# Mask constants copied by DVE and POOL instead of ACT, with a new order of issue, in a sliding-window transformer block

## The chip, the cores and the metric

The kernel runs on one core of one Trainium2 chip. The time is device microseconds of one execution. Before the change it is 662.07 us, the median of 3 runs (661.29 to 662.28).

The engines have short names here: PE is TensorE (matmuls; PEld is its weight load), DVE is VectorE, ACT is ScalarE, POOL is GpSimd, and SP is SyncE, which issues the transfers. "Lnnn" is a line of the kernel before.

## What is computed

The input is 4 sequences of 2,048 rows with 256 features. One block of a transformer is applied: layer normalisation, attention over a sliding window, residual; layer normalisation, a feed-forward net whose weights are rounded to -1, 0 and 1, residual.

```python
def attn(x, Wq, Wk, Wv, Wo):             # 16 heads of 16
    q, k, v = proj(x, Wq), proj(x, Wk), proj(x, Wv)
    allowed = (j <= i) & (j > i - 64)    # 64 keys back
    bias = where(allowed, 0, -inf)
    attn = softmax(q @ k.T * 0.25 + bias)
    return (attn @ v) @ Wo.T

def ffn(x, W1, b1, W2, b2):
    q = lambda W: clip(round(W / (mean(abs(W)) + 1e-5)), -1, 1)
    return relu(x @ q(W1).T + b1) @ q(W2).T + b2

x = hidden
x = x + attn(layernorm(x), Wq, Wk, Wv, Wo)
x = x + ffn(layernorm(x), W1, b1, W2, b2)
```

## The kernel before

**Tiling.** The rows are cut into 32 chunks of 256 (`C`), 8 to a sequence. Each chunk goes through the same stages: load, normalise (`norm_in`), projections to q, k and v (`project`), a stacked operand (`stack`), row maxima (`maxima`), attention weights (`weights`), values (`values`), output projection (`wo_out`), and the two layers of the feed-forward net (`ffn1`, `ffn2`). Precision is kept by splitting a float32 number into a high and a low float16 half: ACT writes the high half, and DVE or POOL subtracts to give the low one.

**The stacks and the mask.** The mask is folded into the matmul of the scores. There are three buffers `st`, used in turn by the chunks (chunk 0, 3, 6 and so on use the first). Each has three planes of 16 heads x 256: plane 0 for the queries, planes 1 and 2 for the keys, at two offsets of the window. Partitions 64 to 111 get the q and k halves of the chunk by transfers (L703). The other partitions hold constants: `qcon` in plane 0 and `kcon` in planes 1 and 2, which make scores outside the window very negative. These constants are written once for each buffer, in `stacks`: 12 copies of 128 x 1024 each (4 for each plane), 36 in all. Before the change ACT makes the copies of plane 1 (L334, 12 in all) and DVE those of planes 0 and 2 (L337, 24 in all). A chunk's transfers into its buffer come after the copies. When they have landed, DVE moves the keys of plane 1 into plane 2 (L714, L716, L719). Then PE computes scores for the maxima (L749), DVE reduces them (L757, twice a chunk), the maxima go through a transpose (L771) and a transfer (L777) into the last row of plane 0, and PE computes the scores again for the exponentials (L792).

**The low half of the weights.** `weights` has two forms. In one, ACT writes the exponentials into a buffer `r` (L802), casts the high half (L805), and POOL subtracts (L807). In the other ACT works in the bank of PSUM (L811, L813) and DVE subtracts (L815). The method `pick` chooses by how loaded the engines are so far.

**The start.** Weights are loaded and prepared while the first chunks are normalised and projected. The feed-forward weights need the mean of their absolute values: four sums on ACT (L460), a matmul (L466), a threshold on DVE (L469 to L472), the rounding on DVE (L482, L484), for the first weight a subtract on POOL (L489) and bias columns copied by POOL (L496), and transposes on PE (L499, L510). Thirty filler tasks of four small matmuls each (L424) keep PE busy when it has nothing else.

**What sets the order.** Nothing is left to a scheduler on the chip. `Lanes` runs the whole program once in a model at build time: each task is a generator which says which engine it needs and for how long (`yield "A", 0.9` is ACT for 0.9 us), which buffer it takes, and what it waits for. Among the tasks that could start, the planner takes the one that starts first (within `TOL`), and among those the one of lowest priority number. That number is made from `PRIO`, `SLOPE` (times the chunk), and `EARLY` for the first three chunks. The order in which the planner picks tasks is the order of the instructions on each engine and in SP's queue, fixed by explicit dependencies. An engine never takes a later instruction first. So a constant of the planner can move any instruction of the kernel; the durations in `yield` are only the planner's assumptions.

Of the kernel before, what the change touches and what calls it, by code (L numbers as in the profile page):

```python
# [19 lines left out]
D = 256  # L20
# [16 lines left out]
PARTS = slice(64, 112)  # L37
R = 113
BIGH = 60000.0
PRIO = {'norm': 23.33, 'proj': 25.05, 'max': 13.47, 'att': 27.65, 'val': -28.15, 'wo': 28.21, 'ffn': -22.66, 'ffn2': 41.64, 'mask': 31.19, 'prep': 14.07}  # L40
SLOPE = {'norm': 0.0, 'proj': 0.024, 'max': 0.0, 'att': 0.045, 'val': -0.116, 'wo': 0.043, 'ffn': 0.052, 'ffn2': -0.228, 'mask': -0.25, 'prep': 0.0}
BUFS = {'xt': 11, 'ln': 2, 'xT': 3, 'zT': 4, 'qk': 2, 'pp': 6, 'op': 2, 'o': 2, 'h': 7, 'r': 5, 'bank': 5, 'lin': 5, 'sp': 1, 'tp': 3, 'pv': 4}
BANKS = ("lin", "tp", "pv")
EARLY = {'norm': (0.0, 0.0, 1.08), 'proj': (0.0, 0.0, 0.0), 'max': (10.44, 0.0, 0.0), 'att': (0.0, 0.0, 0.0), 'val': (0.0, 15.88, 0.0), 'wo': (-6.94, 0.0, 0.0), 'ffn': (10.96, 3.26, -1.28), 'ffn2': (0.0, 2.05, -3.47), 'mask': (0.72, 0.0, 0.0), 'prep': (0.0, 0.0, -1.0)}
TOL = 0.0
FIRST = 0.0
BOOST = 3.34
CHAIN = ('PE', 'DVE', 'Activation', 'Pool', 'SP')
LAT = {"P": 0.2, "A": 0.17, "D": 0.15, "G": 0.13, "S": 0.97}
TAU = 35.06  # L50
DMAF, DLAT = 1.15, 0.83
WINDOW = 3.4133
WT = {'P': 0.93, 'A': 1.17, 'D': 1.05, 'G': 1.07, 'S': 0.0}


class Lanes:
# [21 lines left out]
    def put(self, pool):  # L78
        self.slots[pool].append(self.cur[0])
        self.wake(("get", pool))  # L80
        if pool == "sp":
            self.cur[1] += BOOST
        if pool in BANKS:
            self.cur[1] += BOOST
            self.slots["bank"].append(self.cur[0])
# [11 lines left out]
    def pick(self, options):  # L97

        top = max(self.load[e] * WT[e] for e in "PADG")
        cost = [sum(t * math.exp((self.load[e] * WT[e] - top) / TAU) for e, t in o) for o in options]  # L100
        return cost.index(min(cost))
# [47 lines left out]
    def run(self):  # L149
        while self.ready:  # L150
# [21 lines left out]
            if not could:  # L172
                break
            first = min(x[0] for x in could) + TOL
            start, _, task = min((x for x in could if x[0] <= first), key=lambda x: (x[1], x[0]))
# [4 lines left out]
            if what == "get":  # L180
# [3 lines left out]
                if arg in BANKS or arg == "sp":  # L184
                    task[1] -= BOOST
            elif what == "S":
# [17 lines left out]
def kernel(ctx: ExitStack, tc: tile.TileContext, x, Wq, Wk, Wv, Wo, W1, b1, W2, b2, out):  # L204
    nc = tc.nc
    B, S, _ = x.shape
# [33 lines left out]
    def wait(*key):  # L240
        return ("wait", key)

    def signal(*key):
        lanes.signal(key)
# [3 lines left out]
    def start(kind, c, gen, k=0):  # L248
        early = EARLY[kind][int(c)] if c < 3 else 0.0
        lanes.add(c * (1 + SLOPE[kind]) + PRIO[kind] + early + 0.001 * k, gen)  # L250

# [8 lines left out]
    st = [const.tile([128, 3, H, C], HP, name=f"st{i}") for i in range(NQ)]  # L260
# [66 lines left out]
    def stacks(i):  # L327
        yield wait("masks")
        for k in range(3):
            for h in range(0, H, 4):  # L330
                src = (qcon if k == 0 else kcon[:, k - 1]).unsqueeze(1).to_broadcast([128, 4, C])
                if k == 1:
                    yield "A", 0.9
                    nc.scalar.copy(st[i][:, k, h:h + 4], src)  # L334
                else:
                    yield "D", 0.35
                    nc.vector.tensor_copy(st[i][:, k, h:h + 4], src)  # L337
        signal("used", i - NQ)

# [642 lines left out]
    for i in range(NQ):  # L982
        start("mask", i, stacks(i))
# [28 lines left out]
```

## Time and profile before

| what | value |
|---|---|
| median of 3 runs | 662.07 us (661.29 to 662.28) |
| the profiled execution | 662.08 us |
| its span | 660.3 us |
| mean granted PE clock | 0.987 |
| L334, ACT copies of the mask, 12 | 12.6 us, 1066 ns each, from 15.8 to 37.6 us |
| L337, DVE copies of `kcon`, 12 | 6.6 us, 566 ns each (411 to 1377) |
| L337, DVE copies of `qcon`, 12 | 5.1 us, 472 ns each |
| L757, first reduce of maxima | starts at 43.0 us, the second at 46.7 us |
| first L792, scores for the exponentials | 53.2 us |
| L807, low halves of the weights on POOL, 242 | 283.4 us, 1193 ns each |
| L815, the same on DVE, 14 | 9.3 us, 685 ns each |
| L703, q and k into a stack, 192 transfers | 3.9 us from issue to landing (median) |

The span is the time from the first to the last instruction in the profiled execution; a run's time is 1.8 us longer. The page gives the span in 40 slices of 16.5 us. PE's row shows when the kernel is filled:

```profile
PE   8777789999999999999999999999999999999997
PEclk9978889999999999999999999999999999999999
```

Each digit is the busy share of a slice in tenths, or the granted clock in tenths of full speed. From the seventh slice on (99 us) PE is over 90% busy until the last. Before that it is not, and its clock is granted in part only. In the groups of instructions "<-" stands between what is written and what is read, and the last columns tell the idle time of that engine just before the instructions, with what ended it.

### The profile page before, as it was taken

What the parts mean: (1) busy time and instruction counts of PE and PEld (TensorE: products, weight loads), DVE (VectorE), ACT (ScalarE), POOL (GpSimd) and SP (SyncE); (2) the same over time, 40 slices, a digit from 0 to 9 for tenths busy, and PEclk for the clock granted to TensorE, in tenths of its full rate; (3) what the DMA queues carried; (4) which work ended last, traced back from release to release, by engine and by line L of the source; (5) the groups of instructions that cost most, each with busy time, mean ns of one, the idle gap of its engine ahead of it and who ended that gap; (6) DMA issues with size and microseconds to landing.
All of it is one profiled execution on the core that took longest, in us unless ns stands there. A gap on an engine that the chain in (4) does not pass through costs nothing.

```text
span 660.3 us, 31728 instructions
## 1 busy us (share of the span) xinstructions
PE 626.4 (95%) x13524; PEld 556.2 (84%) x13524; DVE 546.1 (83%) x1145; ACT 534.0 (81%) x1083; POOL 531.5 (80%) x626
## 2 busy tenths in 40 slices
PE   8777789999999999999999999999999999999997
PEld 6656668888899998889988888998898888889986
DVE  7797879987888998888888888889788887878753
ACT  7967788898879886887888789879787978998731
POOL 5355899998979998994998989798969887998630
PEclk9978889999999999999999999999999999999999
DMA  6866478667575878766774755864848776272231
GB/s 184 182 130 135 68 135 150 119 111 142 120 146 110 157 132 123 140 103 141 138 128 97 141 128 113 167 138 99 140 117 148 140 124 142 58 125 65 60 88 49
DMA packets 165037, 81.42 MB, mean 123 GB/s; under 512 B 110880, under 2 KB 162848, under 8 KB 164896
## 3 DMA queue, kind: packets, MB, share of 16 engines
q1 hardware_dynamic: 164896, 79.39, 62.0%
q8 instruction: 106, 1.74, 1.2%
q14 instruction: 35, 0.29, 0.2%
HBM read 11.67 MB, written 8.39 MB: 30 GB/s over the span
## 4 chain that ended last, share of the span: by engine, by line
PE 63%; POOL 12%; DVE 9%; ACT 7%; issue 4%; DMA 3%; SPq 1%; POOLq 0%; ACTq 0%; DVEq 0%
PE bank L917 14%; PE bank L646 8%; PE bank L957 7%; PE bank L958 7%; PE bank L792 6%; POOL pl L807 6%; PE sp L749 5%; PE bank L638 5%; PE bank L882 4%; PE bank L835 3%; PE bank L833 3%; PE bank L834 2%; DVE mx L757 2%; DMA st<-hl 2%; DVE o L851 1%
## 5 line engine op out<-in xcount | busy, mean ns | idle before, releaser
L807 POOL TENSOR_TENSOR pl<-r,ph 128x512 f16<-128x512 f32 x242 | 283.4, 1193 | 23.0 <-ACT ph L805 17.8
L802 ACT ACTIVATE r<-bank 128x512 f32<-128x512 f32 x242 | 137.6, 600 | 23.7 <-PE bank L792 16.0
L805 ACT CAST ph<-r 128x512 f16<-128x512 f32 x242 | 143.7, 629 | 0.8
L917 PE MATMUL bank<-zT,wq 128*128 128x256 f16 x1024 | 125.5, 272 | 0.7 <-DVE o L851 0.7
L957 PE MATMUL bank<-wq,hh 128*128 128x256 f16 x512 | 120.1, 273 | 0.2 <-DVE hl L938 0.2
L757 DVE TENSOR_REDUCE mx<-sp 128x16 f32<-128x1536 f32 x64 | 111.9, 1748 | 10.2 <-PE sp L749 9.9
L958 PE MATMUL bank<-wq,hl 128*128 128x256 f16 x512 | 119.6, 272 | 0.0
L938 DVE SCALAR_TENSOR_TENSOR hl<-bank,hh 128x512 f16<-128x512 f32 x128 | 86.5, 688 | 36.9 <-ACT hh L936 35.5
L917 PEld LDWEIGHTS <-wq 128*128 128x128 f16 x1024 | 97.1, 98 | 12.7 <-DVE o L851 1.2
L936 ACT ACTIVATE hh<-bank 128x512 f16<-128x512 f32 x128 | 75.9, 601 | 31.5 <-PE bank L917 31.2
L792 PE MATMUL bank<-st 114*128 114x64 f16 x2048 | 87.1, 193 | 4.7 <-ACT r L802 2.5
L792 PEld LDWEIGHTS <-st 114*128 114x128 f16 x2048 | 77.6, 98 | 10.0 <-issue 3.3
L833 PEld LDWEIGHTS <-ph 128*128 128x128 f16 x1024 | 82.1, 96 | 4.1 <-DVE o L851 1.0
L834 PEld LDWEIGHTS <-ph 128*128 128x128 f16 x1024 | 80.3, 96 | 4.8 <-issue 3.3
L835 PEld LDWEIGHTS <-pl 128*128 128x128 f16 x1024 | 79.8, 96 | 3.6 <-POOL pl L807 3.3
L851 DVE TENSOR_TENSOR o<-bank,rec 64x128 f32<-64x128 f32 x256 | 73.9, 289 | 8.4 <-POOL rs L542 0.5
L749 PE MATMUL sp<-st 113*32 113x96 f16 (+2 forms) x4608 | 58.7, 202 | 2.8 <-DVE mx L757 1.4
L749 PEld LDWEIGHTS <-st 113*32 113x32 f16 x4608 | 49.2, 96 | 12.1 <-issue 10.5
L683 DVE TENSOR_TENSOR hl<-bank,hl 128x512 f16<-128x512 f32 x64 | 43.8, 689 | 16.6 <-ACT hl L681 15.7
L958 PEld LDWEIGHTS <-hl 128*128 128x128 f16 x512 | 50.0, 98 | 5.0 <-issue 0.3
L957 PEld LDWEIGHTS <-hh 128*128 128x128 f16 x512 | 49.7, 97 | 5.1 <-issue 0.2
L542 POOL TENSOR_TENSOR rs<-rs,mhalf 128x2 f32<-128x2 f32 x64 | 47.1, 736 | 5.3
(118 smaller groups left out, 1518.4 us busy)
## 6 DMA issues: line engine op xcount, KB each, us to landing
st<-hl SPq DMA_DIRECT2D x192, 128.0 KB, 3.9
xt<-in_dram SPq DMA_DIRECT2D x44, 256.0 KB, 4.4
out_dram<-xt SPq DMA_DIRECT2D x32, 256.0 KB, 3.6
ve<-vo SPq DMA_DIRECT2D x32, 136.0 KB, 3.3
ve<-vo SPq DMA_DIRECT2D x60, 68.0 KB, 3.9
oT<-op SPq DMA_TRANSPOSE x64, 3.0
xT<-ht SPq DMA_TRANSPOSE x32, 3.7
st<-mst SPq DMA_DIRECT2D x32, 8.0 KB, 2.3
```

Of the source, the lines that this page charges most:

```text
L749: nc.tensor.matmul(sp[32 * n:32 * n + 32, at:to], st[c % NQ][0:R, 0, h, b * W + q * 32:b * W + q * 32 + 32], window(c, h, b)[0:R, k0:k0 + ...
L757: nc.vector.tensor_reduce(ps_["mx", c][:, w].rearrange("x u p -> x (u p)"), sp.rearrange("x (m k) -> x m k", k=96), AX.X, ALU.max)
L792: nc.tensor.matmul(tp[:, i], window(c, h, b)[0:R + 1], st[c % NQ][0:R + 1, 0, h, b * W:b * W + W], start=True, stop=True)
L802: nc.scalar.activation(pf, tpf, AF.Exp, scale=0.25 / (SW * SW))
L805: nc.scalar.copy(phf, pf)
L807: nc.gpsimd.tensor_tensor(plf, pf, phf, ALU.subtract)
L833: nc.tensor.matmul(pv[:, p, :], ph[:, i, :], v[:, 0, b // 2, p, :], start=True, stop=False)
L834: nc.tensor.matmul(pv[:, p, 0:32], ph[:, i, :], v[:, 1, b // 2, p, 0:32], start=False, stop=False)
L835: nc.tensor.matmul(pv[:, p, :], pl[:, i, :], v[:, 0, b // 2, p, :], start=False, stop=True)
L917: nc.tensor.matmul(ps[:, u], wq1[:, d + d * i, fs], zT[:, i, d], start=n == 0, stop=n == 3)
L957: nc.tensor.matmul(ps[:, t, :], hh[:, f % 2, ts], wq2[:, f, :], start=f == 0, stop=False)
L958: nc.tensor.matmul(ps[:, t, :], hl[:, f % 2, ts], wq2[:, f, :], start=False, stop=f == NF - 1)
```

## The change

It has two parts. In `stacks`, the 12 copies of plane 1 leave ACT: for buffer 0 DVE makes them (4 copies), for buffers 1 and 2 POOL (8 copies). And the planner's constants have other values, so that its order of issue is another throughout.

```diff
-PRIO = {'norm': 23.33, 'proj': 25.05, 'max': 13.47, 'att': 27.65, 'val': -28.15, 'wo': 28.21, 'ffn': -22.66, 'ffn2': 41.64, 'mask': 31.19, 'prep': 14.07}
-SLOPE = {'norm': 0.0, 'proj': 0.024, 'max': 0.0, 'att': 0.045, 'val': -0.116, 'wo': 0.043, 'ffn': 0.052, 'ffn2': -0.228, 'mask': -0.25, 'prep': 0.0}
+PRIO = {'norm': 22.94, 'proj': 25.05, 'max': 12.36, 'att': 27.73, 'val': -26.14, 'wo': 26.43, 'ffn': -22.84, 'ffn2': 39.62, 'mask': 31.7, 'prep': 14.07}
+SLOPE = {'norm': 0.0, 'proj': 0.031, 'max': -0.006, 'att': -0.001, 'val': -0.138, 'wo': 0.105, 'ffn': 0.073, 'ffn2': -0.182, 'mask': -0.25, 'prep': 0.073}
...
-EARLY = {'norm': (0.0, 0.0, 1.08), 'proj': (0.0, 0.0, 0.0), 'max': (10.44, 0.0, 0.0), 'att': (0.0, 0.0, 0.0), 'val': (0.0, 15.88, 0.0), 'wo': (-6.94, 0.0, 0.0), 'ffn': (10.96, 3.26, -1.28), 'ffn2': (0.0, 2.05, -3.47), 'mask': (0.72, 0.0, 0.0), 'prep': (0.0, 0.0, -1.0)}
-TOL = 0.0
+EARLY = {'norm': (1.41, 0.0, 1.08), 'proj': (0.88, 0.27, -1.95), 'max': (10.44, 0.0, 0.0), 'att': (0.0, 0.0, 0.0), 'val': (0.0, 15.66, 0.0), 'wo': (-6.94, 0.0, -5.33), 'ffn': (10.96, 3.26, -1.28), 'ffn2': (0.0, 2.05, -3.47), 'mask': (0.72, 0.0, 0.0), 'prep': (0.0, 0.0, 3.79)}
+TOL = 0.03
 FIRST = 0.0
-BOOST = 3.34
+BOOST = 3.29
...
-TAU = 35.06
-DMAF, DLAT = 1.15, 0.83
+TAU = 34.37
+DMAF, DLAT = 1.14, 0.84
 WINDOW = 3.4133
-WT = {'P': 0.93, 'A': 1.17, 'D': 1.05, 'G': 1.07, 'S': 0.0}
+WT = {'P': 0.95, 'A': 1.19, 'D': 1.05, 'G': 0.96, 'S': 0.0}
...
                 src = (qcon if k == 0 else kcon[:, k - 1]).unsqueeze(1).to_broadcast([128, 4, C])
-                if k == 1:
-                    yield "A", 0.9
-                    nc.scalar.copy(st[i][:, k, h:h + 4], src)
+                if k == 1 and i:
+                    yield "G", 1.3
+                    nc.gpsimd.tensor_copy(st[i][:, k, h:h + 4], src)
                 else:
-                    yield "D", 0.35
+                    yield "D", 0.38 if k == 1 else 0.35
                     nc.vector.tensor_copy(st[i][:, k, h:h + 4], src)
```

`WT` and `TAU` weigh the engines' loads in `pick`: with POOL's weight at 0.96 instead of 1.07, all 256 low halves of the weights go to POOL (L807) and none to DVE (L815). One of 32 second normalisations goes the other way, from POOL and ACT (L580, L581, L584) to DVE (L588). In the number of matmuls nothing changes, and the 120 filler matmuls remain.

## The prediction

> **What bounds the kernel now.** I read the busy shares first, then the same busy times stage by stage, then the chain of waits in order of time.
>
> ```profile
> span 660.3 us, 31728 instructions
> PE 626.4 (95%) x13524; PEld 556.2 (84%) x13524; DVE 546.1 (83%) x1145; ACT 534.0 (81%) x1083; POOL 531.5 (80%) x626
> ```
>
> TensorE (PE) is busy for 95% of the span, so 33.9 us are idle. The stages say where. Columns: stretch, its length, then busy us of PE, PE's weight loads, DVE, ACT, POOL; the granted clock of PE; DMA share; GB/s.
>
> ```profile
> 0.00:16.50 16.50, 13.41 (x96) 9.91 (x96) 13.02 (x45) 12.29 (x35) 8.44 (x26) 1.00 0.64 184
> 16.50:33.00 16.50, 13.19 (x133) 10.87 (x132) 12.93 (x36) 16.50 (x32) 5.61 (x9) 1.00 0.86 182
> 33.00:49.50 16.50, 12.13 (x227) 9.50 (x227) 16.23 (x29) 11.11 (x20) 8.83 (x13) 0.79 0.61 130
> 49.50:66.00 16.50, 13.06 (x311) 10.81 (x315) 11.60 (x21) 12.44 (x27) 9.04 (x10) 0.90 0.63 135
> 66.00:99.00 33.00, 26.04 (x793) 22.77 (x792) 26.41 (x53) 26.54 (x56) 30.20 (x31) 0.90 0.62 102
> 132.00:330.00 198.00, 194.20 (x4337) 175.07 (x4336) 171.84 (x358) 167.56 (x343) 174.75 (x199) 1.00 0.69 130
> 330.00:600.00 270.00, 266.01 (x6151) 238.46 (x6150) 229.01 (x473) 228.06 (x462) 239.36 (x270) 1.00 0.65 124
> ```
>
> From 132 to 600 us PE is idle for 3.80 + 3.99 = 7.8 us of 468: that stretch is bound by PE, and a faster helper gains nothing there. In the first 99 us PE is idle for 21.2 us, and part of its work there is filler (line 424). So a microsecond saved in the head, before PE fills, is a microsecond off the end; the head is where the mask copies lie. There ACT is the full engine from 16.5 to 33 (16.50 of 16.50), and DVE from 33 to 49.5 (16.23 of 16.50). The chain over the first 120 us names the copies; columns are start, length, engine, tile and line:
>
> ```profile
> 15.90 0.93 ACT st L334
> ...
> 27.55 0.63 ACT st L334
> ...
> 28.91 0.93 ACT st L334
> ...
> 30.25 0.93 ACT st L334
> ...
> 36.26 0.93 ACT st L334
> ```
>
> The reader is to see five pieces of line 334 on the chain, 4 x 0.93 + 0.63 = 4.35 us. The other seven copies (of 12) are not on it.
>
> **The change, part by part.**
>
> *Twelve ACT copies go.* Each advances ACT by 0.93 us, so 11.2 us leave ACT, 4.35 us of it from the chain. I don't book 4.35 us, since DVE's order comes next; DVE limits what can be had. DVE works in order. From the threshold step of the first feed-forward weight (line 469, at 17.93 us) to the end of the second maximum of chunk 0 (line 757, ending at 48.43) it takes 30.5 us. In it DVE is idle for 1.09 + 0.41 + 0.51 + 0.16 = 2.2 us, all but 0.16 of it waiting for ACT's line 681. That idle time goes with the copies: -2.2. The step at 17.93 waits for the fourth sum of line 460 on ACT. In the changed order no copy and one weight eviction fewer stand before it (0.93 + 0.27 = 1.2 us). I take half, -0.6, because DVE gets more work before that point (next).
>
> *DVE gets four copies.* They join the chunk-0 stack. A copy takes 0.42 us, and pairs advance by 0.33 (0.75 us for two). In the changed order all eight mask copies of stack 0 are out before the first line 683, while three of the four query copies of stack 2 move behind the threshold. Before the threshold DVE had 0.25 + 0.21 + 1.73 = 2.2 us idle, which covers four more copies (1.3 us) and leaves 0.9; without that cover they cost 1.3. From the threshold to the second maximum I count the instructions in the two issue orders. Line 337 stands 11 times in both, lines 482, 484, 683 and 656 are equal, one batch of statistics (lines 537 and 539, 1.03 us) moves behind, two steps of line 387 (0.4) move ahead, and two of line 567 (0.8) come in: -0.6 us.
>
> *POOL gets eight copies.* The trace has no such copy on POOL. POOL's one-input selects give 0.41 us for 256 elements (line 316) and 0.62 for 512 (line 320), so 0.82 ns an element and 1.04 us for 1,024. The two-input subtract of line 489 takes 1.04 us at least for 512, so 2.1 us is the upper bound. A copy has one input, so I take 1.04: 8.3 us in all (16.7 by the upper bound). POOL idles for 8.45 us before 20.16, then 2.72, 2.59 and some smaller gaps, so its own time is covered for the first four. The last four stand ahead of the third line 489 and of the scaling of chunk 3, and push chunk 3's transposed input about 1 us back, to 40.3 us. Its projection stands behind the first transpose of maxima (line 771), which came at 48.84 us, so this is covered.
>
> What isn't covered is the meeting of POOL and DVE:
>
> ```profile
> 32.03 1.38 DVE L337 COPY st<-kcon 128x1024 f16<-128x1024 f16 x1
> ...
> 34.39 0.41 DVE L337 COPY st<-kcon 128x1024 f16<-128x1024 f16 x1
> ```
> ```profile
> 31.78 1.34 POOL L559 TENSOR_TENSOR ht<-r,ht 128x512 f16<-128x512 f32 x1 [0.64 <-ACT ht L557]
> ```
>
> The first DVE copy ends 0.29 us after the POOL subtract ends at 33.12; the second, with no long POOL work beside it, takes 0.41. It happens again at 38.32 (1.27 us). From 20 to 50 us POOL runs eight long subtracts (four each of lines 489 and 559), and these two meetings cost 0.96 + 0.85 = 1.8 us: 0.23 us a subtract. For the first four POOL copies that is 0.9 us, covered by the 0.9 us left above. For the last four it is +0.9. The bounds are 0 and 4 x 1.04 = 4.2 for each four.
>
> The Trainium skill, "SBUF — State Buffer", "Who interferes with whom", speaks against this part: it says that GpSimd and a VectorE copy in a two-port mode hold one pair of ports in turn, each for its whole instruction, and that the second to come is blocked, not slowed. The rows above agree where the two meet (1.38 and 1.27 us against 0.42). Were each of the eight copies to block DVE for its whole length, the sum would end at about 666 instead of 659.8; the 0.23 us measured per subtract is what decides here.
>
> *The new order of SyncE's queue.* Chunk 1's transpose is no longer second in its pair: its second half (line 564) stands behind all four sums, and the transfer behind the four loads of the second weight (3.24 us) and an input load (0.47). Up to 5 us late; chunk 1's projections follow, with 32 filler matmuls now ahead of them. The cover: chunk 1's stack transfers (line 703) went out at 41.29, 12 us after their data was ready at 29.4, queued behind chunk 3's transpose and a value transfer. Now they stand ahead of both, and chunk 0's six ahead of its value transfer. If the cover failed, the 5 us would come through. I book nothing, since DVE's order (above) sets when the landed stack is used.
>
> *Fourteen subtracts leave DVE.* All 256 low halves of the weights are now made by POOL (line 807), 14 of them formerly by DVE (line 815):
>
> ```profile
> L807 POOL TENSOR_TENSOR pl<-r,ph 128x512 f16<-128x512 f32 x242 | 283.4, 1193 | 23.0 <-ACT ph L805 17.8 <-issue 2.2 <-PE bank L835 1.1
> L815 DVE TENSOR_TENSOR pl<-bank,ph 128x512 f16<-128x512 f32 x14 | 9.3, 685 | 1.0 <-ACT ph L813 0.8
> ```
>
> POOL gains 14 x 1.193 = 16.7 us, DVE loses 9.3, ACT is even within 0.6. From 132 to 600 POOL is busy 414.1 of 468 us (88%); with all 16.7 in it, 92%. PE and its weight loads now wait 2.3 + 3.3 us for line 807, 0.023 us each: 14 more give +0.3. Bounds: 0, and 16.7 if each were on PE's path. One late normalisation moves from POOL and ACT to DVE (two instructions); PE is full there (20.00 of 20 from 600 to 620), so it is nothing.
>
> **The sum.** -2.2 - 0.6 - 0.6 + 0.9 + 0.3 = -2.2 us. What follows the second maximum shifts as a whole: from 66 to 99 POOL is the fullest engine (30.20 of 33), and nothing of the change touches its work there. The profiled execution took 662.08 us, 1.8 more than its span and 0.01 off the median of 662.07. Forecast: **659.8 us**.
>
> **The rivals.** *More than that.* PE runs at 0.90 of its clock from 49.5 to 99, after idle gaps; that is 0.1 x 49.5 = 5 us. An order with fewer gaps takes some. For it: these gaps are waits for the same late stacks. Against: fillers are as many as before and are used up earlier. With the whole 4.35 of the chain and a third of the 5 us: 656.1.
>
> *Hidden anyway.* DVE stays the bound of the head, and the four late POOL copies cost it the 2.8 us that ACT's waits and the lighter order gave back. For it: 16.23 of 16.50. It ends at 661.8.
>
> *Slower: POOL becomes the late engine.* Place: the low halves of line 807 from 66 us on. POOL is already at 92% from 66 to 99, and it loses its 14 reliefs. If a third of the 16.7 us comes back as PE's waits, 5.6 us against a head gain of 2.5 gives 665.2. It decides once POOL's share from 132 to 600 passes about 95%, where a late subtract can't be caught up within a chunk. Against it: 88% now, PE waits of only 2.3 us for line 807, and room from 300 to 320 us (12.40 of 20 busy).
>
> That the edit doesn't do what it says is excluded for the copies by the changed program: no copy of line 334 is left on ACT.
>
> **How the numbers follow.** Forecast 0.37 (657.5 to 660.7), more than that 0.15, hidden 0.20, slower 0.28. About 0.2%, or 1.3 us, is what a measurement of this kernel can tell from no change. So faster is 0.37 + 0.15 = 0.52, same 0.20, slower 0.28. The range goes from the large gain, 656.0, to the slower rival, 665.5; the latter also holds the case of both fours of POOL copies blocking DVE in part. The likeliest case's own range is 657.5 to 660.7.
>
> **What would show it.** In the changed profile: ACT below 16.5 of 16.5 from 16.5 to 33 us; POOL copies near 1.04 us; the second maximum of chunk 0 ending near 46 us instead of 48.4, and the first matmul of line 792 near 51 instead of 53.2; DVE copies of 1 us or more at most four times; POOL near 92% and PE idle under 9 us from 132 to 600. I am wrong if line 792 starts no earlier, if POOL copies take 2 us, or if PE waits for line 807 by several us more.

## The result and the profile after

The changed kernel takes 670.66 us, the median of 4 runs (669.62 to 672.59). The kernel before takes 662.17 us beside it (661.29 to 663.67). The ratio is 1.0121, with a 95% interval of 1.0096 to 1.0147: the change makes the kernel 1.2% slower. The forecast was 659.8 us, and its range ended at 665.5. The profiled execution took 670.13 us, its span is 668.4 us, 8.1 more than before.

First the page of the changed kernel: the busy shares, PE's row and its clock in 40 slices of 16.7 us, and the group of line 807.

```profile
span 668.4 us, 31755 instructions
...
PE 628.5 (94%) x13524; PEld 558.1 (84%) x13524; DVE 549.2 (82%) x1137; ACT 523.0 (78%) x1069; POOL 554.7 (83%) x646
...
PE   7866979999999999999999999999999999999997
...
PEclk9978899999999999999999999999999999999999
...
L807 POOL TENSOR_TENSOR pl<-r,ph 128x512 f16<-128x512 f32 x256 | 300.4, 1196 | 19.6 <-ACT ph L805 10.7
```

ACT has lost the 11 us of the copies, as meant (534.0 to 523.0). POOL gained 23.2 us. PE is idle for 668.4 - 628.5 = 39.9 us instead of 33.9, and it is busy for 2.1 us more, with the same matmuls. Some of these were slower in the first 23 us: 28 filler matmuls from 13.61 us take 4.47 us (32 took 3.46 from 13.09 us before), and 16 take 2.51 us from 19.76 us but 1.70 from 28.59. Together, idle and busy, that is the 8.1 us. The same busy times by stretch (columns: stretch, length, busy us of PE, PE's weight loads, DVE, ACT, POOL, PE's granted clock, DMA share, GB/s) say where:

```profile
16.50:33.00 16.50, 14.63 (x129) 11.61 (x127) 13.59 (x44) 9.36 (x24) 4.13 (x6) 1.00 0.69 145
33.00:49.50 16.50, 10.43 (x144) 8.22 (x145) 15.12 (x24) 6.99 (x13) 11.70 (x14) 0.79 0.51 100
49.50:66.00 16.50, 11.03 (x331) 8.69 (x330) 12.42 (x22) 11.29 (x25) 8.25 (x11) 0.85 0.60 119
66.00:99.00 33.00, 28.16 (x757) 24.64 (x754) 26.45 (x59) 27.89 (x60) 30.68 (x32) 0.92 0.66 120
...
132.00:330.00 198.00, 194.77 (x4452) 175.25 (x4450) 172.49 (x355) 168.44 (x345) 180.49 (x209) 1.00 0.69 129
330.00:600.00 270.00, 261.78 (x5989) 234.74 (x5989) 224.84 (x460) 222.04 (x449) 234.48 (x265) 1.00 0.67 124
```

ACT did come free from 16.5 to 33 us: 9.36 of 16.5 instead of 16.50. Yet PE lost in two places. From 33 to 66 us it is busy for 21.46 us instead of 25.19. From 330 to 600 us it is busy for 261.78 instead of 266.01, so 4.2 us more are idle in a stretch that the prediction took as bound by PE. POOL from 132 to 600 is busy for 415.0 us, as much as before (414.1): the fourteen added subtracts did not fill it.

**The head.** The timelines of DVE and of POOL in the changed kernel (start, length, engine, line; x2 stands for two instructions shown as one) show POOL's copies meeting DVE:

```profile
5.07 5.39 DVE L337 COPY st<-qcon 128x1024 f16<-128x1024 f16 x8
...
14.09 1.14 DVE L337 COPY st<-kcon 128x1024 f16<-128x1024 f16 x1
...
15.15 1.26 DVE L337 COPY st<-qcon 128x1024 f16<-128x1024 f16 x1
...
24.83 0.69 DVE L683 TENSOR_TENSOR hl<-bank,hl 128x512 f16<-128x512 f32 x1 [2.11 <-ACT hl L681]
...
35.13 0.78 DVE L482 TENSOR_SCALAR r<-xt,thr 128x512 f16<-128x512 f32 x1
35.94 1.52 DVE L484 SCALAR_TENSOR_TENSOR r<-xt,thr,r 128x512 f16<-128x512 f32 x1
...
38.74 1.27 DVE L482 TENSOR_SCALAR r<-xt,thr 128x512 f16<-128x512 f32 x2
39.93 1.40 DVE L484 SCALAR_TENSOR_TENSOR r<-xt,thr,r 128x512 f16<-128x512 f32 x2
41.37 1.68 DVE L719 COPY st<-st 48x3072 f16<-48x3072 f16 x1
...
47.78 1.75 DVE L757 TENSOR_REDUCE mx<-sp 128x16 f32<-128x1536 f32 x1
...
51.17 1.75 DVE L757 TENSOR_REDUCE mx<-sp 128x16 f32<-128x1536 f32 x1
```
```profile
8.16 2.02 POOL L334 COPY st<-kcon 128x1024 f16<-128x1024 f16 x2
13.92 2.21 POOL L334 COPY st<-kcon 128x1024 f16<-128x1024 f16 x2
...
34.59 1.03 POOL L334 COPY st<-kcon 128x1024 f16<-128x1024 f16 x1
35.88 3.45 POOL L334 COPY st<-kcon 128x1024 f16<-128x1024 f16 x3
40.75 1.48 POOL L489 TENSOR_TENSOR r<-r 128x512 f16<-128x512 f16 x1 [1.42 <-DVE r L484]
```

The same places on DVE in the kernel before:

```profile
5.08 3.42 DVE L337 COPY st<-qcon 128x1024 f16<-128x1024 f16 x8
...
17.93 0.16 DVE L469 TENSOR_REDUCE thr<-bank 128x1 f32<-128x4 f32 x1 [1.73 <-PE bank L466]
...
37.33 0.96 DVE L719 COPY st<-st 48x3072 f16<-48x3072 f16 x1
...
43.04 1.72 DVE L757 TENSOR_REDUCE mx<-sp 128x16 f32<-128x1536 f32 x1
```

The eight copies of `qcon` took 3.42 us before and take 5.39 now, 2.0 us more: that is the length of the first two POOL copies (2.02 us). One of the eight, 0.42 us long elsewhere, takes 2.48 us: it waits for both. The next two POOL copies stretch two DVE copies to 1.14 and 1.26 us, and 1.6 us are lost. The last four stretch other DVE instructions: line 484 from 0.74 to 1.52 us, and line 482 twice, from 0.47 to 0.78 and to 0.88 (the first of the two at 38.74 us), 1.5 us in all. Line 719 goes from 0.96 to 1.68 us, but beside a subtract of POOL (line 489, from 40.75 us); POOL's copies had ended at 39.33. The maxima of chunk 0 (line 757) start at 47.78 and 51.17 us instead of 43.04 and 46.68. ACT shows the way from the first copies to there:

```profile
17.17 0.38 ACT L384 ACTIVATE wkh<-bank 128x256 f16<-128x256 f32 x1 [0.91 <-DVE wkl L387]
...
24.21 0.59 ACT L681 CAST hl<-bank 128x512 f16<-128x512 f32 x1 [4.56 <-PE bank L646]
```

DVE is late, so its small parts of the weights (line 387) are late, and ACT waits for them at 17.17 us (last column: idle time before, and what ended it). Behind that stand the last two sums of line 460, at 17.93 and 18.54 us, and so the threshold (line 469) comes at 19.94 us instead of 17.93. Behind the threshold's matmul stand 16 filler matmuls on PE (2.51 us from 19.76 us), and only then chunk 0's q projection, at 22.07. In the kernel before only eight stand there. So ACT gets that projection at 24.21 instead of 20.45 us, after 4.56 us of waiting. The ACT that was set free waits, and DVE waits for it in turn: from the threshold to the end of the second maximum DVE is idle for 3.8 us (2.11 + 0.49 + 1.08 + 0.16), where the kernel before had 2.2.

**The steady state.** This is what PE waits for from 132 to 600 us in the changed kernel (line, releaser, total us, times, longest us), and below it the one such row of the kernel before in the same stretch that says "issue", which means that PE waited for nothing that the profile shows:

```profile
PE bank L792 <- issue: 2.1, 2, 1.1
...
PE bank L833 <- issue: 1.4, 3, 0.6
...
PE bank L882 <- issue: 1.1, 1, 1.1
PE sp L749 <- issue: 1.0, 2, 0.5
...
PE bank L834 <- issue: 0.4, 1, 0.4
```
```profile
PE sp L749 <- issue: 1.3, 2, 0.7
```

That is 6.0 us at nine places against 1.3 us at two: 4.7 of the 8.1 us. One of the nine, in PE's timeline:

```profile
400.08 0.27 PE L882 MATMUL bank<-wol,oT 128*128 128x256 f16 x1
400.19 0.38 PE L882 MATMUL bank<-woh,oT 128*128 128x256 f16 x2
401.69 0.27 PE L882 MATMUL bank<-wol,oT 128*128 128x256 f16 x1 [1.12 <-issue]
401.80 0.38 PE L882 MATMUL bank<-woh,oT 128*128 128x256 f16 x2
```

PE stops for 1.12 us in the middle of a run of equal matmuls with the same operands. Late data is unlikely there. Count PE's instructions in the order of its program: 27,048 matmuls and weight loads, and 105 others that the trace shows (nearly all are waits for a semaphore). The nine places are rows 16,320, 16,576, 17,344, 18,113, 18,881, 19,648, 22,208, 23,744 and 24,001. The steps between them are 1, 3, 3, 3, 3, 10, 6 and 1 times 256, each to within one row. The transfers between 396 and 402 us, by queue (packets, MB, share of 16 engines):

```profile
q1 hardware_dynamic: 989, 0.85, 83.5%
q8 instruction: 1, 0.02, 1.8%
```

One packet of 16 KB on the queue of instructions came beside 989 packets of data. Over the whole execution that queue carries 106 packets, 1.74 MB; 27,153 / 256 is 106.1. So PE's program arrives in blocks of 256 instructions, and PE stops where a block isn't there in time.

The traces of all nineteen kernels (the two and the seventeen below) bear this out. PE stops 100 times for 0.15 us or more with no releaser, and each time at row 192 or 193 of a count by 256, whichever work stands there. Of its 531 waits behind 60 us that have a releaser, ten stand at such a row. The packets tell the same: one stands ahead of each edge of a block, and at none of 1,995 edges did PE go on sooner than 1.2 us after the end of that packet. At the 100 stops it went on 1.2 to 1.9 us after it (1.3 to 1.7 at the nine). The 256 instructions before a stop had run in 2.9 to 4.9 us (median 3.5), those before the other edges in a median of 5.7. So a block tends to be late where PE runs quickly through the one before it.

The Trainium skill, "Advanced Engine Details and Errata", "ISA Cache", states the same block (16 KB, 256 instructions); the steps and the packets agree.

### The profile page after: what moved, and what is told of

Its sections match the earlier page's. It is cut to its first block, busy times and chain, and to the rows that moved or that the text cites. A ratio compares the mean times of both kernels' runs of the same rounds, so it can differ in the third digit from the quotient of the medians.

```text
span 668.4 us, 31755 instructions
## 1 busy us (share of the span) xinstructions
PE 628.5 (94%) x13524; PEld 558.1 (84%) x13524; DVE 549.2 (82%) x1137; ACT 523.0 (78%) x1069; POOL 554.7 (83%) x646
## 3 DMA queue, kind: packets, MB, share of 16 engines
q8 instruction: 106, 1.74, 1.2%
## 5 line engine op out<-in xcount | busy, mean ns | idle before, releaser
L807 POOL TENSOR_TENSOR pl<-r,ph 128x512 f16<-128x512 f32 x256 | 300.4, 1196 | 19.6 <-ACT ph L805 10.7
L802 ACT ACTIVATE r<-bank 128x512 f32<-128x512 f32 x256 | 144.2, 602 | 41.6 <-PE bank L792 36.2
L805 ACT CAST ph<-r 128x512 f16<-128x512 f32 x256 | 152.8, 633 | 0.7
```

The costliest lines, as they stand in the source:

```text
L802: nc.scalar.activation(pf, tpf, AF.Exp, scale=0.25 / (SW * SW))
L805: nc.scalar.copy(phf, pf)
L807: nc.gpsimd.tensor_tensor(plf, pf, phf, ALU.subtract)
```

## The experiments

Seventeen kernels were run. The expectations name these theories: A, POOL's copies hold DVE up and cost the time; B, the new order costs it and the copies help; C, any order other than the one before is worse, since that one was selected; D, the constants or the edit are bad by themselves; E, late blocks of PE's code; F, the time of the fillers ahead of chunk 0's projections. Ratios are to the kernel before, run beside each.

### The two halves, on each order

`plan_before_copies_moved`: the order of the kernel before, unchanged, with the copies on the engines of the change (lines behind 337 are three higher there).

```diff
                     yield "A", 0.9
-                    nc.scalar.copy(st[i][:, k, h:h + 4], src)
+                    if i:
+                        nc.gpsimd.tensor_copy(st[i][:, k, h:h + 4], src)
+                    else:
+                        nc.vector.tensor_copy(st[i][:, k, h:h + 4], src)
```

> The order of issue of the kernel before is kept to the instruction; the 12 copies of plane 1 stand at the same places of that order but run on DVE (buffer 0) and POOL (buffers 1 and 2). Theory A (the copies on POOL block DVE and cost the time): slower than before, by 2 to 6 us (664 to 668). Theory B (the new order costs the time, the copies help): at or below before, 658 to 662, since ACT is relieved.

Measured: 666.28 us, ratio 1.0063 [1.0030, 1.0096]. DVE's timeline and POOL's in this kernel:

```profile
34.77 1.52 DVE L487 SCALAR_TENSOR_TENSOR r<-xt,thr,r 128x512 f16<-128x512 f32 x1
...
37.36 1.44 DVE L487 SCALAR_TENSOR_TENSOR r<-xt,thr,r 128x512 f16<-128x512 f32 x1
38.83 1.68 DVE L722 COPY st<-st 48x3072 f16<-48x3072 f16 x1
...
46.98 1.72 DVE L760 TENSOR_REDUCE mx<-sp 128x16 f32<-128x1536 f32 x1
```
```profile
34.51 1.23 POOL L335 COPY st<-kcon 128x1024 f16<-128x1024 f16 x1
37.22 2.48 POOL L335 COPY st<-kcon 128x1024 f16<-128x1024 f16 x2
```

Line 487 is line 484 of the kernel before (0.74 us alone), 722 is 719 (0.96), 760 is 757. Between 27 and 43 us ten DVE instructions are stretched by 6.9 us in all. In the kernel before three are, by 2.0 us (0.96, 0.85 and 0.19), beside POOL's subtracts. So with the seven POOL copies of that time 4.9 us more are lost, 0.7 us a copy; this is a net figure, as some of the ten stand beside POOL's subtracts, which moved too. The threshold comes 1.0 us earlier than before (16.97 us), since ACT is free; that part was right. The first maximum comes 4.9 - 1.0 = 3.9 us later, at 46.98. The later reduces of maxima stand 3.1 to 5.8 us behind the kernel before, the last 4.1: what is lost in this head is still lost at the end. Theory A holds on this order.

`plan_after_copies_on_dve`: the order of the changed kernel, with the eight POOL copies on DVE.

```diff
                     yield "G", 1.3
-                    nc.gpsimd.tensor_copy(st[i][:, k, h:h + 4], src)
+                    nc.vector.tensor_copy(st[i][:, k, h:h + 4], src)
```

> The order of issue of the changed kernel is kept; the 8 copies that POOL makes run on DVE at the same places. Theory A: no DVE copy is stretched beyond 1 us by them, the second maximum of chunk 0 starts 3 us or more earlier than 51.2 us, and the time falls by 3 us or more, to 667 or less. Theory B: the time stays within 2 us of 670.7.

Measured: 668.45 us, 1.0083 [1.0054, 1.0112]. The threshold is back at 17.52 us and the first maximum at 45.18, 2.6 us earlier than in the changed kernel, but 2.1 later than before, as the fillers still stand ahead of chunk 0's projections. Of the 8.5 us only 2.2 are gone, less than theory A told and more than theory B: POOL's copies are a part. Even of the 2.6 us nothing is left at 372 us; what this kernel gains comes behind that (see the table below).

`copies_alone` (the edit of `stacks` with the constants of before, planned anew) and `constants_alone` (the new constants with the copies as before):

```diff
-                if k == 1:
-                    yield "A", 0.9
-                    nc.scalar.copy(st[i][:, k, h:h + 4], src)
+                if k == 1 and i:
+                    yield "G", 1.3
+                    nc.gpsimd.tensor_copy(st[i][:, k, h:h + 4], src)
...
-                    yield "D", 0.35
+                    yield "D", 0.38 if k == 1 else 0.35
```

> Only the edit in the stacks, with the planner's constants of before, so the planner makes its own order for it. Theory A: slower than before by 3 us or more (665 or more). Theory B: 660 to 663. A third theory C (any order other than the one of before is worse, whatever the edit): 664 to 672 without a stretched DVE copy in the head being needed.

> Only the planner's constants of the change; the copies stay on ACT and DVE as before. Theory A: close to before, 660 to 664. Theory B: near the changed kernel, 668 to 672. Theory C: 664 to 672.

Measured: 679.55 us, 1.0251 [1.0219, 1.0283], and 675.99 us, 1.0188 [1.0156, 1.0220]. Each half alone is worse than both. The first lies above the ranges of theories B and C, the second above all three. Since the planner makes a new order in each, this tells nothing about the halves until it is known what a new order by itself does.

### Is any new order dear?

Three edits that should do nothing. `placebo_0p36` changes one assumed duration by 0.01 us in the kernel before; `pick_weights_alone` takes over `TAU` and `WT` alone; `placebo_after_dma` sets `DMAF, DLAT` of the changed kernel back.

```diff
-                    yield "D", 0.35
+                    yield "D", 0.36
```
```diff
-TAU = 35.06
+TAU = 34.37
...
-WT = {'P': 0.93, 'A': 1.17, 'D': 1.05, 'G': 1.07, 'S': 0.0}
+WT = {'P': 0.95, 'A': 1.19, 'D': 1.05, 'G': 0.96, 'S': 0.0}
```
```diff
-DMAF, DLAT = 1.14, 0.84
+DMAF, DLAT = 1.15, 0.83
```

> Before, with one number of the planner's model changed from 0.35 to 0.36 us (the assumed time of a DVE copy); no instruction runs on another engine by this edit itself, but the planner makes another order. Theory C (the order of before is a selected one, and any other order costs time): ratio 1.01 to 1.025, like the copies alone (1.025) and the constants alone (1.019). Theory D (the constants or the edit are bad in themselves): ratio within 0.3% of 1.

> Before, with only TAU and WT of the change: all 256 low halves go to POOL. If POOL's extra 16.7 us are what costs, ratio 1.01 or more with PE waiting for line 807 by 5 us more than before (2.3 us); by theory C, 1.01 to 1.025 without that wait.

> The changed kernel, with two numbers of the planner's model of transfers back at their old values (1.15, 0.83). Theory C: the constants of the change are a selected set for the new edit, so that any other order costs time: ratio to before 1.02 to 1.03, 1% or more above the changed kernel. If the changed kernel's order is an ordinary one: as likely below 1.012 as above.

Measured: 681.31 us, 1.0282 [1.0252, 1.0311]; 678.00 us, 1.0229 [1.0193, 1.0265]; 671.16 us, 1.0128 [1.0077, 1.0179]. A change of 0.01 us in an assumption costs 19 us. Its loss lies in more than one stage, as three stretches show against those of the kernel before:

```profile
66.00:99.00 33.00, 24.11 (x644) 20.35 (x641) 26.74 (x49) 22.33 (x48) 23.63 (x27) 0.81 0.52 102
...
132.00:330.00 198.00, 190.05 (x4430) 169.80 (x4427) 172.03 (x355) 167.95 (x341) 173.69 (x201) 1.00 0.70 127
330.00:600.00 270.00, 264.31 (x5882) 237.20 (x5881) 226.15 (x465) 222.10 (x451) 226.33 (x263) 1.00 0.71 126
```

PE's 24.11, 190.05 and 264.31 stand against 26.04, 194.20 and 266.01. Five kernels with new orders were 1.3 to 2.8% slower, whatever was edited. The changed kernel, at 1.2%, is at the good end of them. So theory C holds for the kernel before. The fourteen added subtracts are not what costs in `pick_weights_alone`: PE waits 2.2 us for line 807 there, 2.3 before. For the order of the changed kernel it missed: its neighbour `placebo_after_dma` is about as fast as itself. From here on only kernels with a kept order are compared.

`plan_before_copies_on_dve` (all twelve copies on DVE) and `plan_before_buffer0_on_dve` (only the four of buffer 0), in the order of before:

```diff
-                    nc.scalar.copy(st[i][:, k, h:h + 4], src)
+                    nc.vector.tensor_copy(st[i][:, k, h:h + 4], src)
```
```diff
-                    nc.scalar.copy(st[i][:, k, h:h + 4], src)
+                    (nc.scalar.copy if i else nc.vector.tensor_copy)(st[i][:, k, h:h + 4], src)
```

> The order of before, all 12 copies of plane 1 at their places but on DVE. If POOL's copies blocked DVE for about their whole length (7 us of stretched DVE work were seen with them on POOL, against 3 us that ACT's relief gave back), this runs 3 us or more faster than the same order with 8 of them on POOL: ratio to before 0.995 to 1.002, and no DVE copy of plane 1 over 0.6 us. If it was the loss of ACT as a helper, the ratio stays at 1.006.

> The order of before, only the four copies for buffer 0 on DVE, the other eight stay on ACT. DVE has idle time there, ACT is full: 1 to 2 us faster than before (ratio 0.997 to 0.9985) if a saving in the head carries to the end; 1.000 if it doesn't.

Measured: 663.13 us, 1.0019 [0.9999, 1.0039], and 662.61 us, 0.9998 [0.9973, 1.0022]. With all twelve on DVE, 3.2 of the 4.2 us that `plan_before_copies_moved` had lost come back, as theory A told (one copy is still stretched, to 1.37 us). Yet taking the copies off ACT brings nothing against the kernel before, and the second expectation missed. With four on DVE the first maxima come 1.2 us earlier, and 0.4 us of it is left at the end of the profiled executions.

### What the order of the changed kernel costs

`plan_after_buffer1_on_dve` puts the first four of POOL's copies on DVE; `plan_after_fewer_fillers` leaves out the 16 filler matmuls ahead of chunk 0's projections (they make nothing of the output).

```diff
-                    nc.gpsimd.tensor_copy(st[i][:, k, h:h + 4], src)
+                    (nc.gpsimd if i == 2 else nc.vector).tensor_copy(st[i][:, k, h:h + 4], src)
```
```diff
-    def filler():
+    def filler(n):
...
-        for i in range(4):
+        for i in range(0 if 18 <= n < 22 else 4):
...
-        start("prep", 300, filler(), i)
+        start("prep", 300, filler(i), i)
```

> The order of the changed kernel; only the four POOL copies for buffer 1, which stand at 8.2 and 13.9 us, run on DVE at their places, the four for buffer 2 (34.6 to 39.3 us) stay on POOL. If the first four are what blocks (a DVE copy of 2.48 us beside them), the first matmul of line 792 comes 2 to 3 us earlier than 58.7 us and the ratio falls from 1.012 to about 1.009; if the last four do, the ratio stays at 1.012.

> The order of the changed kernel, without the 16 filler matmuls that stand between the first threshold and chunk 0's projections (2.5 us in its profile). If these fillers hold up the projections, line 681 of chunk 0 starts 1.5 to 2.5 us earlier than 24.2 us and the time falls by about as much, to 668 to 669.5; if the projections wait for something else, or lose the clock that the fillers keep up, no change (670 to 672).

Measured: 666.17 us, 1.0056 [1.0026, 1.0087], and 666.44 us, 1.0064 [1.0042, 1.0086]. Each brings about half of the loss back, more than was told, but little of it by the head. In the first, line 792 starts 4.1 us earlier (54.67 us) and the first maximum 2.4; at 372 us 0.6 us of that is left, at the last reduce it is 3.5 us ahead. In the second, line 681 starts 1.7 us earlier, as told, but its first maximum comes only 0.65 us earlier than in the changed kernel, and at 372 us it is still 0.6 us ahead; at the end it is 5.5 us ahead. The gain falls between 395 and 600 us, where the stalls of PE are. That led to theory E: leaving out 16 matmuls and their weight loads moves the blocks of 256 against the work by 32.

### Blocks of code or fillers

The same edit of `filler` with other conditions: `after_last_fillers_dropped` (`n >= 26`: 16 matmuls behind chunk 0's projections), `after_eight_fillers_dropped` (`n >= 22`: 32 matmuls), `before_last_fillers_dropped` (`n >= 26` in the kernel before), `after_early_fillers_dropped` (`12 <= n < 16`: ahead of the threshold).

```diff
-        for i in range(4):
+        for i in range(0 if n >= 26 else 4):
```

> The changed kernel without the 16 filler matmuls of the last four filler tasks (PE at 28.59 us, 1.70 us of them); the 16 fillers ahead of chunk 0's projections stay. Every other instruction keeps its place. Theory E (code blocks): PE's program arrives in blocks of 256 instructions, and PE stops where a block is late. In the changed kernel PE idles 6.0 us between 132 and 600 us with nothing it waits for, at nine places, all of which lie a whole number of such blocks apart (kernel before: 1.3 us at two places). Dropping 32 instructions (16 matmuls, 16 weight loads) moves the blocks against the work exactly as in plan_after_fewer_fillers, where these stalls came to 1.7 us. So this run gives 666 to 668 (ratio about 1.007) with at most 3 us of such stalls, though chunk 0 gets no earlier. Theory F (the fillers' own time ahead of chunk 0's projections is what plan_after_fewer_fillers gained): the fillers of that place are still there, so nothing is gained: 670 to 671, ratio 1.012, stalls of about 6 us.

> The changed kernel without the last eight filler tasks (32 matmuls, 64 instructions of PE). Another phase of the code blocks: 64 of 256. Theory E: the stalls lie on the same rows of PE's program (about row 16,226 plus multiples of 256), at other work than in the changed kernel, and their sum is again not 6.0 us; the time goes with that sum within 1.5 us (665 to 670). Theory F: 669 to 671, as nothing ahead of chunk 0's projections is changed; stalls near 6 us.

> The kernel before without the 16 filler matmuls of the last four filler tasks (PE at 28.5 us). Every other instruction keeps its place. Theory E: the phase of the code blocks moves by 32 instructions here too. The kernel before has only 1.3 us of stalls between 132 and 600 us; if that is a lucky phase, this run gets 3 to 5 us of them and comes to 664 to 666 (ratio 1.003 to 1.006). If stalls stay under 2 us, the kernel before is little exposed in any phase, and its time stays at 661.5 to 663. A theory without code blocks says 661.5 to 662.5: PE waits there for other work in any case.

> The changed kernel without 16 filler matmuls of the group at 13.61 us, ahead of the first threshold; all later fillers stay, everything else keeps its place. Theory E (code blocks): the phase is that of plan_after_fewer_fillers and after_last_fillers_dropped, whose stalls between 132 and 600 us were 1.69 and 1.67 us (with no shift 6.02, 3.67 and 2.57 in three kernels): 1.4 to 2.2 us here, all on the same rows. If the head keeps the times of the changed kernel within 1 us (the reduces of maxima at 300 us), the time is 665.5 to 667.5, ratio 1.005 to 1.0075. If the phase does nothing and only the head counts: stalls of 3 us or more, 669 to 671 with an unchanged head.

And both cures together: `after_buffer1_and_fillers` has the edits of `plan_after_buffer1_on_dve` and `plan_after_fewer_fillers`; `after_copies_on_dve_and_fillers` has all twelve copies on DVE and the same 16 fillers left out.

> The order of the changed kernel with the first four POOL copies on DVE (670.7 to 666.2 alone) and without the 16 fillers ahead of chunk 0's projections (666.4 alone). If the first acts on the head and the second on the code blocks, the gains add in part: the head gives 2.5 us, the blocks the 3.7 us of stalls that are left in plan_after_buffer1_on_dve less about 1.7: 664 to 665, ratio 1.004. If both have taken away the same stalls between 395 and 450 us, nothing adds: 666, ratio 1.006. Under 662 would beat the kernel before.

> The order of the changed kernel with all twelve copies on DVE and without the 16 fillers ahead of chunk 0's projections. after_buffer1_and_fillers (POOL keeps the four copies of buffer 2) took 664.23. Theory A (POOL's copies hold DVE up wherever they meet): the last four gone from POOL too, 1 to 2 us less: 662 to 663.5, ratio 1.000 to 1.0015, stalls of code blocks near 1.6 us. If the four of buffer 2 cost nothing once the head is early: 664 to 665, as they then only swap 4 x 1.03 us of POOL for 4 x 0.42 us of DVE, which is the fuller engine from 33 to 49.5 us. Under 661.5 would beat the kernel before.

Measured:

| kernel | us | ratio, interval |
|---|---|---|
| `after_last_fillers_dropped` | 669.64 | 1.0115 [1.0088, 1.0143] |
| `after_eight_fillers_dropped` | 670.80 | 1.0127 [1.0094, 1.0160] |
| `before_last_fillers_dropped` | 664.46 | 1.0032 [1.0012, 1.0052] |
| `after_early_fillers_dropped` | 668.72 | 1.0091 [1.0065, 1.0117] |
| `after_buffer1_and_fillers` | 664.23 | 1.0024 [1.0005, 1.0044] |
| `after_copies_on_dve_and_fillers` | 663.42 | 1.0022 [1.0002, 1.0043] |

By their totals the first two and the fourth missed theory E, and the fourth by its stalls too (2.5 us). The traces say why. All these kernels have the order of the changed one, so the n-th reduce of maxima can be compared with its n-th. The table gives this difference at 372 us and at the last reduce (599.6 us in the changed kernel), the difference of the two, and PE's stalls without a releaser between 132 and 600 us, all of profiled executions:

| order of the changed kernel | at 372 us | at the end | between | stalls | less 6.0 |
|---|---|---|---|---|---|
| changed kernel | 0 | 0 | 0 | 6.0 | 0 |
| `plan_after_copies_on_dve` | +0.4 | -3.0 | -3.4 | 2.6 | -3.4 |
| `plan_after_buffer1_on_dve` | -0.6 | -3.5 | -2.9 | 3.7 | -2.3 |
| `plan_after_fewer_fillers` | -0.6 | -5.5 | -5.0 | 1.7 | -4.3 |
| `after_last_fillers_dropped` | +4.0 | -0.6 | -4.6 | 1.7 | -4.3 |
| `after_eight_fillers_dropped` | +2.3 | 0.0 | -2.3 | 4.3 | -1.7 |
| `after_early_fillers_dropped` | +4.3 | +0.7 | -3.6 | 2.5 | -3.5 |
| `after_buffer1_and_fillers` | -3.1 | -7.4 | -4.3 | 1.6 | -4.4 |
| `after_copies_on_dve_and_fillers` | -2.7 | -6.6 | -3.9 | 2.5 | -3.5 |

The last column (the stalls less the 6.0 us of the changed kernel) gives the column "between" to about 0.6 us in all eight. So what these kernels gain in the steady state is in the main the stalls. Three of them lost 2 to 4 us in the head for leaving out fillers elsewhere, which hid that gain. In two of these 1.4 us of the loss is another such stall, on line 749 at 64 us; the rest was not traced. The last two kernels bring the head back as well, and only both cures together do: each alone left at most 0.6 us of its gain at 372 us, together they leave 3.1. Why the two need each other was not traced. Whether POOL or DVE copies for buffer 2 makes no difference that can be told (664.23 and 663.42 us). Here are the threshold and the maxima of chunk 0 on DVE in `after_buffer1_and_fillers`, and the first eviction of the projection on ACT:

```profile
17.51 0.16 DVE L469 TENSOR_REDUCE thr<-bank 128x1 f32<-128x4 f32 x1
...
43.29 1.75 DVE L757 TENSOR_REDUCE mx<-sp 128x16 f32<-128x1536 f32 x1
...
46.78 1.76 DVE L757 TENSOR_REDUCE mx<-sp 128x16 f32<-128x1536 f32 x1
```
```profile
18.84 0.58 ACT L681 CAST hl<-bank 128x512 f16<-128x512 f32 x1 [1.41 <-PE bank L646]
```

The maxima are within 0.3 us of where the kernel before has them (43.04 and 46.68), the threshold and the eviction stand ahead of it. With both cures the order of the changed kernel is 0.2% slower than the kernel before, at the edge of what can be told. No kernel of the seventeen beats the kernel before.

Is it the phase of the blocks against the work that decides? With no shift the stalls were 6.0, 3.7 and 2.6 us in three kernels, with a shift of 32 they were 1.7, 1.7, 2.5, 1.6 and 2.5, with 64 they were 4.3. The ranges all but touch, so this is likely but not settled. That the stops are late blocks is shown by their rows and by the packets; how long PE stops at a row differs between kernels with the same phase, and why was not traced. What makes a block late was not tried by itself. The kernel before has 1.3 us of stalls, and 1.8 with a shift of 32, so it isn't much exposed; its 0.3% in that run come in small steps from 184 us on and were not traced.

## Why the prediction was wrong

The prediction had +0.9 for the meetings of POOL and DVE, -3.4 for DVE's and ACT's gains, nothing for the order, and +0.3 for the subtracts (662.07 - 2.2 is 659.9, written as 659.8). Step by step:

- *"For the first four POOL copies that is 0.9 us, covered by the 0.9 us left above."* This step failed. The first four cost 2.0 + 1.6 us of DVE time, and behind DVE's line 387 ACT waited with the sums. The "-0.6" for an earlier threshold became +2.0. With those four on DVE the threshold came at 17.5 us and the first maximum 2.4 us earlier. The run gained 4.5 us, but most of that is shorter stalls of PE behind 372 us, which is luck of the order and not this step.
- *"The 0.23 us measured per subtract is what decides here."* It was two meetings spread over eight subtracts. (The copy at 34.39 us, read there as one with no long POOL work beside it, had line 542 beside it, 1.27 us from 33.57 us on 128x2 elements, and took 0.41.) The last four POOL copies were to cost 0.9 us by it and cost DVE 1.5. Seven cost 4.9 us in the order of before, 0.7 us each, and the first two of the changed kernel 1.0 us each, their whole length. The Trainium skill, "SBUF — State Buffer", "Who interferes with whom", said so (the second to come is blocked for the whole instruction), and the prediction set 666 beside it as what that would give. The copies alone, in an unchanged order, gave 666.3. That the two figures agree is luck in part, as 0.7 us a copy is less than the whole length.
- *"That idle time goes with the copies: -2.2."* ACT came free as told, but line 681 waited for PE instead of for ACT: PE had 16 fillers ahead of chunk 0's projections. Without them line 681 comes 1.7 us earlier. DVE's idle time rose from 2.2 to 3.8 us instead of going to nothing. The prediction counted the fillers ahead of chunk 1's projections and not those.
- *"I book nothing, since DVE's order (above) sets when the landed stack is used"*, of SyncE's new order. Chunk 0, ahead of chunk 1, came late already, and by PE's and DVE's order. Its second maximum was to end near 46 us and ends at 51.17 + 1.75 = 52.9; the first matmul of line 792 was to come near 51 and comes at 58.73 (53.19 before). With both cures chunk 0's maxima are back and that matmul still comes at 54.91; whether SyncE's order is behind these 1.7 us was not traced.
- *"That stretch is bound by PE, and a faster helper gains nothing there"*, of 132 to 600 us, with +0.3 for line 807. In the prediction's own count (PE and its weight loads, whole execution) the waits for line 807 rose from 2.3 + 3.3 to 3.6 + 4.9 us, which is 2.9 instead of 0.3; but from 132 to 600 us they did not rise (PE 1.3 and 1.2, weight loads 2.1 and 2.0). The large term was in no part of the sum, and this is the step that failed by most: late blocks of PE's own code, 6.0 instead of 1.3 us, so +4.7 where the prediction had nothing.
- *"So a microsecond saved in the head, before PE fills, is a microsecond off the end"*. It held for a loss (3.9 us at the first maximum, 4.1 at the last, in the order of before) and not for what was saved: 1.2 us of `plan_before_buffer0_on_dve` were 0.4 at the end, and 2.4 us of `plan_after_buffer1_on_dve` were 0.6 at 372 us.
- What was right: the POOL copy (1.04 us told, 1.03 us measured at the median); mask copies of 1 us or more on DVE at most four times (four, but other DVE work was held up as well); POOL from 132 to 600 (told 92%, measured 88.7%) is no late engine, so the rival that would have given 665.2 isn't what happened, though its sign was right.

The account of the 8.1 us of span, by `after_buffer1_and_fillers`: 3.1 us in the head (what both cures bring back by 372 us), 4.3 us of stalls (what they bring back from there to the last reduce), and 661.2 - 660.3 = 0.9 us of span that is left with both cures: together 8.3. The first term is for both cures as a pair; the runs don't split it between POOL's copies and the fillers.

## What to carry to other kernels

A copy moved to POOL is free for POOL and may still stop DVE for its whole length: look at what DVE does beside it, and at what waits for DVE. In a kernel whose order of issue is planned and selected, an edit that makes the planner run anew can cost 1 to 3% by itself (five of five did here), so test an edit with the order held. And where PE stops in mid-run with no releaser, count its instructions between the stops before looking for late data.

## What the hardware did that was not expected

One DVE copy of 0.42 us waited through two POOL copies that stood back to back (2.48 us): DVE did not get a turn between them. It was not copies alone: the `tensor_scalar` of line 482, which turns float32 into float16, went from 0.45 to 1.26 us beside a POOL copy (in `plan_before_copies_moved`, line 485 there), and the `scalar_tensor_tensor` of line 484 with two inputs in SBUF from 0.74 to 1.52. Line 683, which reads PSUM, took its usual 0.68 us at 34.52 us with POOL's copy from 34.59 beside it. PE's stalls at the edges of its blocks of code reached 2.0 us in one case (`after_early_fillers_dropped`, line 917), in a stretch where PE is otherwise full.
